# Gate and routing of the last batch ahead of the early experts, and four early experts in place of eight

## The chip, the cores and the metric

The kernel runs on one core of one Trainium2 chip. The metric is the device time of one execution in microseconds; the time of a kernel is the median of its runs. The core has five engines with a queue each, which run their instructions in the order of the program: TensorE (PE, matrix products and transposes), VectorE (DVE), ScalarE (ACT), GpSimd (POOL) and SyncE (SP). Transfers are issued by SP, ACT or POOL. A transfer with row numbers (an indirect gather or scatter) is issued by POOL.

## What is computed

Four batches of 512 tokens with 512 features pass through four layers, each added to its input. The first two are a quantized expert layer and a feed-forward layer whose weights come out of a table of 16 values. The third is a selective scan over the sequence: for each batch and feature it runs a recurrence with 16 states along the tokens, and the result is multiplied by a gate made from the normalized `x`. The fourth, which the change concerns, is a mixture of 32 experts:

```
probs = softmax(x @ gate_w)
w, sel = top_k(probs, 8);  w = w / sum(w)
pos = position of each (token, expert) pair within its expert, in order of tokens
t_slot, w_slot = token and weight of each slot of each expert
xg = x_pad[t_slot]
y  = (silu(xg @ w_gate[e]) * (xg @ w_up[e])) @ w_down[e]
out[t_slot] += w_slot * y
```

Each expert has matrices of 512x192 (gate and up) and 192x512 (down). With 2048 tokens and 8 experts for each there are 16384 pairs, 512 on average for an expert.

## The kernel before

`tile_kernel` writes the program from Python generators. `weave` takes steps of several generators in turn, in proportion to a number of steps given for each, so that their instructions are mixed in the order of the program. From that order a scheduler at build time makes the queue of each engine. It takes an instruction that stands later in the program when it reckons an engine to be free before an earlier one is ready. On the chip each queue runs in the order so made, and an instruction that waits holds up all that stand behind it on its engine.

The feed-forward layer and the scan of the batches fill the time up to about 1079 us. Batch `b`'s gate (`gate`, L599) and routing (`route`, L696) come once its scan is over, mixed with the scan of batch `b + 1`. For the last batch there is no later scan.

- `gate`: statistics of `x`, per feature block a normalization and a tanh on ACT (L607, L609) and two products on DVE (L610, L612), then transposes on PE (L616, tile `pt_y`) and an addition into `x` on DVE (L618). Statistics (`ln_stats`, L96) end on POOL, with a power and a product (L108, L109).
- `route`, first part: statistics, then four turns, one for every 128 tokens. Each normalizes on ACT (L705, by `normalize` at L114, tile `xn_r`, with a single buffer), stores the rows to the table `xln` in memory (L708, issued by SP), stores `x` to `kept` (L709), transposes on PE (L712), copies on ACT (L714), makes the logits on PE (L717) and copies them on ACT (L724).
- `route`, second part: softmax and the eight largest on DVE (L732 to L755), and the weights to `xln` (L758).
- `place` (L761): positions by products with a triangle and with ones (L772, L773), then four turns that make a table of slots: ACT copies (L795), DVE compares (L797, L804), ACT scales (L811), PE multiplies 32 small blocks (L814), DVE adds into the table (L821).
- `slots` (L826) and `slot_tokens` (L845) turn the tables into row numbers on DVE (L840, L842, L856 to L859). The gathers of the experts read these.

Tables are two: one for the tokens of the first two batches, one for those of the last two. The first `EARLY` experts are visited twice: once with up to 320 slots of the first half's tokens, for which batches 2 and 3 needn't be routed, and a second time with up to 320 slots of the second half's. All other experts have one visit with up to 576 slots, with tokens of both halves. A flag and a branch at the end do the layer again in full if the room was too small.

`expert` (L872) has four steps: SP loads the weights (`egu`, L881 to L883; `ed`, L888 and L890; three buffers) and POOL gathers the rows (L895, tile `xg`, ten buffers, 128 rows each); ACT copies the weights of the rows (L911, `gates`) and PE transposes them (L908, copied by ACT and DVE at L910); PE makes gate and up (L920, tile `pg`), and ACT and DVE the activation (L936 to L938, `eh`); PE makes the down projection (L949, L953, `po_e`), ACT or DVE weights it (L962, L960, `ey`), and POOL scatters it with addition into two tables `sums` (L963). `pipeline` (L972) runs these so that the loads of one expert, the transposes of the next and the products of another are mixed.

After the last scan the early experts' first visits are mixed with the last gate and routing, over the same PSUM banks as the scan (two banks for gate and up, two for transposes and down projections). Then the banks are laid out anew (four and four), and the late list begins, with the experts after `EARLY` in full and the second visits put between them; the last `LAST` = 2 second visits stand at the end, where the sums are read back and added to `x` (`add_sums`, L988).

Of the kernel before, what the change touches and what calls it, by code (L numbers as in the profile page):

```python
# [28 lines left out]
NB = 4  # L29
# [4 lines left out]
KH = HID // P  # L34
# [12 lines left out]


SLOTS = 576
EARLY = 8  # L50
ROOM = (320, 320)
AHEAD = 7
LAST = 2
# [8 lines left out]
class Kernel:  # L62
# [560 lines left out]
    def routing_constants(self, rp):  # L623
# [32 lines left out]
        for g, n in enumerate(ROOM):  # L656
            nc.vector.memset(self.room[:, g, :EARLY], float(n))
        self.no_row = c.tile([P, 1], F32, name="no_row", bufs=1)
# [37 lines left out]
    def route(self, rp, b):  # L696
# [53 lines left out]
        if b == NB // 2:  # L750
            nc.vector.memset(self.seen[0][:, :EARLY], 0.0)

# [275 lines left out]
def run(steps):  # L1028
    for _ in steps:
        pass  # L1030


def staggered(gens, starts):

    gens = list(zip(starts, gens))
    step = 0
    while gens:
        for g in [g for g in gens if g[0] <= step]:
            if next(g[1], StopIteration) is StopIteration:
                gens.remove(g)  # L1040
            else:
                yield
        step += 1


def weave(*streams):

    streams = [[0, n, g] for g, n in streams]
    while streams:
        s = min(streams, key=lambda s: s[0] / s[1])  # L1050
        s[0] += 1
        if next(s[2], StopIteration) is StopIteration:
            streams.remove(s)


@with_exitstack
def tile_kernel(ctx: ExitStack, tc: tile.TileContext, t: dict):
    k = Kernel(tc, t)
    k.constants(ctx)
    scan = ExitStack()  # L1060
    with ExitStack() as early:
        with ExitStack() as ffn:
            wp = ffn.enter_context(tc.tile_pool(name="wp", bufs=1, side="right"))
            with ExitStack() as first:
                k.banks(first, t=2, m=2, y=2, d=2)
                ap = first.enter_context(tc.tile_pool(name="ap", bufs=2))
                sq = staggered([k.smooth_quant(ap, b) for b in range(NB)], (0, 8, 23, 38))
                with ExitStack() as lut:
                    lc = lut.enter_context(tc.tile_pool(name="lc", bufs=1, side="right"))
                    lp = lut.enter_context(tc.tile_pool(name="lp", bufs=2, side="right"))  # L1070
                    k.lut_tables(lc, wp)
                    lookups = k.lut_weights(lp, k.jobs)
                    weave((islice(sq, 49), 49), (islice(lookups, 48), 48))
                    k.tile_rows(wp, lc)
                    weave((islice(sq, 59), 59), (lookups, 4 * len(k.jobs) - 48), (k.scratch(lc), 18))

                pp = ffn.enter_context(tc.tile_pool(name="pp", bufs=1, side="right"))
                k.scan_weights(pp)
                k.prep_tag = "y"
                preps = 2 * KH + 1  # L1080
                weave((k.prepare(pp, pp, 0), preps), (sq, 33))
            k.banks(early, t=2, m=2, y=1, d=3)
            k.prep_tag = "t"
            bp = ffn.enter_context(tc.tile_pool(name="bp", bufs=2, side="right"))
            rp = ctx.enter_context(tc.tile_pool(name="rp", bufs=1))
            mp = scan.enter_context(tc.tile_pool(name="mp", bufs=2))
            k.routing_constants(rp)
            steps = (TPB // 2) * (NIC + 3)
            units = KH * 16
            routes = 2 * (TPB + 1)  # L1090

            ffn_ = chain(*(k.lut_ffn(bp, b) for b in range(NB)))
            run(islice(ffn_, 4))
            for b in range(NB):
                n = steps
                streams = [(k.scan(mp, b), units), (islice(ffn_, n), n)]
                if b + 1 < NB:
                    streams.append((k.prepare(pp, (pp, mp)[(b + 1) % 2], b + 1), preps))
                if b:
                    run(k.gate(mp, b - 1))  # L1100
                    streams.append((k.route(rp, b - 1), routes))
                if b == NB - 1:
                    tok = k.slots(rp, k.tables[:1], 0, EARLY, ROOM[0], "a")
                    at = k.slot_tokens(rp, tok, ROOM[0], "a")
                weave(*streams)
        ep = ctx.enter_context(tc.tile_pool(name="ep", bufs=2, side="right"))
        k.gu_tag = "m"
        full, nc = SLOTS // P, tc.nc
        two = [k.sums[j % 2] for j in range(full + 1)]
        first = k.pipeline(k.expert(ep, e, (k.xln[0], *at, 0), e, ROOM[0], two) for e in range(EARLY))  # L1110
        weave((chain(k.gate(mp, NB - 1), k.route(rp, NB - 1)), KH + routes), (first, 2 * EARLY))
    scan.close()
    k.banks(ctx, t=4, g=4)
    k.gu_tag = "g"
    tp = ctx.enter_context(tc.tile_pool(name="tp", bufs=6))
    at = k.slot_tokens(rp, k.slots(rp, k.tables, EARLY, NE, SLOTS, "u"), SLOTS, "u")
    at_b = k.slot_tokens(rp, k.slots(rp, k.tables[1:], 0, EARLY, ROOM[1], "b"), ROOM[1], "b")
    k.overflow(rp)
    calls = [(e, at, e - EARLY, SLOTS) for e in range(EARLY, NE)]
    for e in range(EARLY - LAST):  # L1120
        calls.insert(2 * e + 1, (e, at_b, e, ROOM[1]))

    calls += [(e, at_b, e, ROOM[1]) for e in range(EARLY - LAST, EARLY)]
    sums = [two] * (len(calls) - LAST) + [k.sums[2:] * 3] * LAST
    late = k.pipeline(
        k.expert(ep, e, (k.xln[1], *at, 0), col, n, s) for (e, at, col, n), s in zip(calls, sums)
    )
    run(islice(late, 2 * (len(calls) - LAST)))
    weave(
        (late, 2 * LAST),  # L1130
        (
            chain(k.add_sums(tp, k.sums[:2], 0, NT // 2, True), k.add_sums(tp, k.sums[:2], NT // 2, NT, False)),
            NT // 2,
        ),
    )
    run(k.add_sums(tp, k.sums[2:], NT // 2, NT, True))
    more = nc.values_load(k.more[0:1, 0:1], min_val=0, max_val=1)
    with tc.If(more):
        k.in_full(rp, ep, tp)
# [51 lines left out]
```

## Time and profile before

| what | value |
|---|---|
| median of 3 runs | 1939.13 us (1932.53 to 1949.87) |
| the profiled execution's own time | 1929.09 us |
| its span, first to last instruction | 1926.9 us |
| mean granted clock of TensorE | 0.939 |
| PE busy with products | 1654.5 us, 86% of the span |
| DVE, ACT, POOL busy | 60%, 37%, 51% |
| transfers | 351.94 MB, 183 GB/s |

The profile is of one execution. Busy times are those of instructions that compute; a PE product's end is modelled. "PEld" is the load of the stationary operand, which overlaps products. `L920` is line 920. In a line of the timeline, the first two numbers are start and length in us, "x16" the number of instructions merged into it, and the brackets hold the idle time of the engine just before it and what ended that. Where a line stands for several, its length is that of the whole group. The granted clock is a share of full speed.

### The profile page before, as it was taken

The page shows a single profiled execution, that of the slowest core. Times are in us where ns is not written, and L with a number is a line of the kernel's source. Part 1 is how long each engine was busy: PE and PEld are TensorE (multiplying, and loading weights), DVE is VectorE, ACT ScalarE, POOL GpSimd, SP SyncE. Part 2 cuts the span into 40 slices and gives each one's busy share as a digit, 9 for nine tenths or more (in the row PEclk, how much of TensorE's full clock was granted, in tenths as well). Part 3 has the DMA queues.
Part 4 walks back from the last instruction along what each step waited for, and adds up shares of the span by engine and source line. Part 5 has one row for each costly group of instructions (what it writes and reads, how often), then busy time and mean ns, then how long its engine had stood idle before and what let it go on. Part 6 is the DMA issues. An engine that isn't in the chain of part 4 may idle for free. (4 is left out here: it accounts for less than half of the span.)

```text
span 1926.9 us, 25051 instructions
## 1 busy us (share of the span) xinstructions
PE 1654.5 (86%) x8845; PEld 981.0 (51%) x8845; DVE 1164.4 (60%) x2025; ACT 715.7 (37%) x1361; POOL 990.0 (51%) x844
## 2 busy tenths in 40 slices
PE   5778775798979898889799588899999999999981
PEld 3444332555455655455555244455656566665640
DVE  6877974688799879888889533523222223232333
ACT  1554555535444554355433332222222222222210
POOL 3110213768746775578466542456555555555421
PEclk9979996899999998999899699899999999999995
DMA  8525620889888788778899785688887777778766
GB/s 246 158 89 178 219 61 35 216 200 221 219 211 202 193 230 213 191 192 226 202 221 220 182 219 127 154 190 185 180 184 172 184 172 166 161 171 190 148 156 223
DMA packets 190363, 351.94 MB, mean 183 GB/s; under 512 B 41827, under 2 KB 88259, under 8 KB 190229
## 3 DMA queue, kind: packets, MB, share of 16 engines
q1 hardware_dynamic: 147844, 253.00, 48.9%
q0 software_dynamic: 39952, 92.66, 23.9%
q10 hardware_dynamic: 2432, 4.59, 0.7%
q8 instruction: 72, 1.18, 0.3%
q14 instruction: 63, 0.51, 0.1%
HBM read 279.17 MB, written 79.47 MB: 186 GB/s over the span
## 5 line engine op out<-in xcount | busy, mean ns | idle before, releaser
L963 POOL DMA_INDIRECT sums<-ey,to x168 | 261.6, 1557 | 299.9 <-DMA sums<-ey,to 122.6
L920 PE MATMUL pg<-exT,egu 128*128 128x320 f32 (+1 forms) x1536 | 403.4, 421 | 10.0 <-DVE exT L910 4.6
L569 POOL TENSOR_TENSOR dBu<-d,BC 128x512 f32<-128x512 f32 x256 | 325.7, 1280 | 118.1 <-DMA d<-dts 67.1
L920 PEld LDWEIGHTS pg<-exT,egu 128*128 128x128 f32 x1536 | 291.3, 193 | 125.8 <-issue 34.7
L574 DVE TENSOR_TENSOR_SCAN st<-st,dBu 128x512 f32<-128x512 f32 x192 | 230.4, 1216 | 37.8 <-POOL dBu L569 36.3
L567 ACT ACTIVATE st<-d,A 128x512 f32<-128x512 f32 x256 | 174.2, 690 | 195.8 <-DVE sc L575 118.8
L895 POOL DMA_INDIRECT xg<-xln,tokens x168 | 162.1, 965 | 101.1 <-PE pt_g L908 43.2
L381 PE MATMUL pgu<-xT,wg 128*128 128x256 f32 (+1 forms) x704 | 182.3, 401 | 15.8 <-DVE h L391 11.2
L937 DVE SCALAR_TENSOR_TENSOR eh<-eh,pg 64x128 f32<-64x128 f32 (+5 forms) x144 | 61.2, 425 | 214.9 <-ACT eh L936 213.8
L949 PE MATMUL po_e<-ed,eh 128*128 128x512 f32 (+1 forms) x336 | 171.3, 630 | 17.8 <-DVE eh L938 9.4
L381 PE MATMUL pgu<-xT,wu 128*128 128x256 f32 (+1 forms) x704 | 177.4, 394 | 0.0
L346 PE MATMUL pw<-oh,lut_t 128*32 128x344 bf16 (+1 forms) x2052 | 126.2, 363 | 58.4 <-DVE oh L340 58.0
L962 ACT ACTIVATE ey<-po_e,gates 128x512 f32<-128x512 f32 (+1 forms) x104 | 68.7, 684 | 281.1 <-PE po_e L953 140.8
L381 PEld LDWEIGHTS pgu<-xT,wg 128*128 128x128 f32 (+1 forms) x704 | 130.4, 195 | 78.9 <-issue 29.9
L960 DVE TENSOR_SCALAR ey<-po_e,gates 128x512 f32<-128x512 f32 x64 | 45.8, 747 | 204.5 <-PE po_e L953 204.5
L397 PE MATMUL po_f<-wd,h 128*128 128x512 f32 (+1 forms) x352 | 157.6, 603 | 2.7 <-DVE h L391 2.2
L381 PEld LDWEIGHTS pgu<-xT,wu 128*128 128x128 f32 (+1 forms) x704 | 135.8, 195 | 25.0 <-issue 4.2
L575 DVE TENSOR_TENSOR sc<-st,BC 128x512 f32<-128x512 f32 x192 | 127.4, 680 | 22.7 <-PE py L585 21.9
L579 POOL TENSOR_TENSOR sc<-sc,BC 128x512 f32<-128x512 f32 x64 | 81.7, 1276 | 100.2 <-DVE sc L572 75.7
L936 ACT ACTIVATE eh<-pg 64x128 f32<-64x128 f32 (+5 forms) x144 | 54.5, 384 | 157.3 <-PE pg L920 144.0
L953 PE MATMUL po_e<-ed,eh 64*128 64x512 f32 (+1 forms) x336 | 112.8, 635 | 0.0
L346 PEld LDWEIGHTS <-lut_t 128*32 128x32 bf16 x2052 | 57.5, 104 | 104.7 <-issue 58.4
(259 smaller groups left out, 2177.7 us busy)
## 6 DMA issues: line engine op xcount, KB each, us to landing
d<-dts SPq DMA_DIRECT2D x256, 512.0 KB, 6.4
egu<-in_w_gate SPq DMA_DIRECT2D x40, 384.0 KB, 4.2
sums<-zero SPq DMA_DIRECT2D x16, 768.0 KB, 6.5
ix<-idx_b SPq DMA_DIRECT2D x16, 688.0 KB, 6.0
egu<-in_w_up SPq DMA_DIRECT2D x40, 256.0 KB, 5.6
ed<-in_w_down SPq DMA_DIRECT2D x40, 256.0 KB, 3.8
ed<-in_w_down SPq DMA_DIRECT2D x80, 128.0 KB, 3.7
acc<-sums SPq DMA_DIRECT2D x20, 512.0 KB, 9.4
```

The costliest lines, as they stand in the source:

```text
L346: nc.tensor.matmul(pt[i][32 * c : 32 * c + 32, :step], lhsT=self.lut_t[:, j, g, :], rhs=oh[:, c * n + i * step : c * n + (i + 1) * step], ...
L381: nc.tensor.matmul(pg[:m, j * W : (j + 1) * W], lhsT=w[:, k, c * P : c * P + m], rhs=xT[:, k, :], start=k == 0, stop=k == KH - 1,)
L397: nc.tensor.matmul(po, lhsT=h[:m, c, i * P : (i + 1) * P], rhs=self.wd[:m, c, :], start=c == 0, stop=c == NIC - 1,)
L567: nc.scalar.activation(st, d[:, 0, :], AF.Exp, scale=self.A[:, i : i + 1])
L569: product = nc.gpsimd.tensor_tensor(dBu, d[:, 1, :], BC[:, 0, :], ALU.mult)
L574: nc.vector.tensor_tensor_scan(st, st, dBu, 0.0, ALU.mult, ALU.add)
L575: nc.vector.tensor_tensor(sc, st, BC[:, 1, :], ALU.mult)
L895: nc.gpsimd.indirect_dma_start(out=xg[:m, :], out_offset=None, in_=xln, in_offset=bass.IndirectOffsetOnAxis(ap=tokens[:m, lo + j, col : co ...
L920: nc.tensor.matmul(pg[i][:, :hs], lhsT=w[:, k, i * P : (i + 1) * P], rhs=xT[:, k, z : z + hs], start=k == 0, stop=k == KH - 1,)
L949: nc.tensor.matmul(po[j][:m, :], lhsT=h[:, 0, b : b + m], rhs=wd[:, 0, :], start=True, stop=False)
L953: nc.tensor.matmul(po[j][:m, :], lhsT=h[r : r + R, 1, b : b + m], rhs=wd[r : r + R, 1, :], start=False, stop=True)
L963: nc.gpsimd.indirect_dma_start(out=sums[j], out_offset=bass.IndirectOffsetOnAxis(ap=to[:m, lo + j, col : col + 1], axis=0), in_=y[:m, :], ...
```

## The change

`EARLY` is 4 and not 8, and the gate and the routing of the last batch stand wholly before the early experts in the program, in place of being woven with them.

```diff
-EARLY = 8
+EARLY = 4
@@
         two = [k.sums[j % 2] for j in range(full + 1)]
         first = k.pipeline(k.expert(ep, e, (k.xln[0], *at, 0), e, ROOM[0], two) for e in range(EARLY))
-        weave((chain(k.gate(mp, NB - 1), k.route(rp, NB - 1)), KH + routes), (first, 2 * EARLY))
+
+        run(chain(k.gate(mp, NB - 1), k.route(rp, NB - 1), first))
```

`EARLY` is also the number of second visits and the first expert of the late list, so experts 4 to 7 change from two visits of 320 slots to one of 576. The late list then has 28 full visits and 4 second ones, where it had 24 and 8. Of the second visits two stand between the first full ones and two at the end (six and two before).

The scheduler still puts some of the early experts' instructions ahead of later routing. In the changed program, PE has all of gate and routing first; ten transposes of the first early expert stand before the 32 blocks of the last table turn, and no other expert product stands ahead of these. ACT has nine copies of `gates` (L911), for the first three experts, ahead of the first normalization of routing. POOL has ten gathers ahead of the power (L108) of the routing's statistics. SP has the loads of experts 0 and, in part, 1 first, then the four stores to `kept`, the rest of expert 1's loads and those of expert 2 between the four stores of normalized rows.

## The prediction

> **What bounds the kernel now.** I read the page's slices first: TensorE (PE) is nine tenths busy or more from slice 27 to 38, after a dip just past the middle. Then I cut the span at the stages the change touches, and read there the chain of waits, the order on each engine, and the transfers.
>
> ```profile
> PE   5778775798979898889799588899999999999981
> PEclk9979996899999998999899699899999999999995
> ```
>
> That dip (slice 23 is 5 tenths, the next three 8) is the edit's place: the scan has ended and the experts start. Busy time by stretch (columns: stretch, length, PE, PEld, DVE, ACT, POOL, granted clock, DMA share, GB/s):
>
> ```profile
> 1079.00:1098.40 19.40, 6.08 (x25) 3.07 (x26) 8.12 (x15) 7.25 (x14) 11.28 (x12) 0.50 0.68 178
> 1098.40:1236.00 137.60, 119.57 (x572) 65.15 (x572) 56.43 (x171) 38.38 (x96) 51.30 (x42) 0.96 0.72 173
> 1256.50:1468.90 212.40, 210.21 (x825) 124.26 (x824) 61.49 (x122) 57.88 (x153) 121.69 (x98) 1.00 0.83 184
> 1468.90:1840.00 371.10, 371.10 (x1485) 228.21 (x1484) 108.20 (x203) 93.30 (x250) 209.04 (x165) 1.00 0.77 168
> ```
>
> From 1256 PE is the only bound: 371.10 of 371.10 us, then 86.9 us of tail. So the late experts cost exactly their PE time. The chain of waits gives the pitch:
>
> ```profile
> 1396.54 1.91 PE po_e L949 x4
> ...
> 1431.36 1.91 PE po_e L949 x4
> ...
> 1600.51 1.91 PE po_e L949 x4
> ...
> 1622.43 1.92 PE po_e L949 x4
> ```
>
> A full expert (576 slots) takes 1622.43 - 1600.51 = 21.92 us; a full one and a second visit of 320 slots take 1431.36 - 1396.54 = 34.82, so a second visit is 12.90. Before that, the timeline of PE:
>
> ```profile
> 1084.12 1.12 PE L616 MATMUL pt_y<-ident,u 128*128 128x128 f32 x4 [2.75 <-DVE u L612]
> ...
> 1098.44 7.22 PE L920 MATMUL pg<-exT,egu 128*128 128x320 f32 x16
> ...
> 1109.36 1.98 PE L949 MATMUL po_e<-ed,eh 128*128 128x512 f32 x4
> ...
> 1115.73 4.47 PE L920 MATMUL pg<-exT,egu 128*128 128x320 f32 x16
> ...
> 1225.84 1.98 PE L949 MATMUL po_e<-ed,eh 128*128 128x512 f32 x4 [0.28 <-DVE eh L938]
> ...
> 1235.46 0.16 PE L868 MATMUL pc<-flag,ones 128*128 128x1 bf16 x1 [3.73 <-ACT ey L962]
> ```
>
> The eight early experts start at 1098.44 and their down projections (L949) run from 1109.36 to 1225.84; gate and routing hide between them. The first late down projection is at 1256.48 by the same timeline. That is my yardstick.
>
> **The change, part by part.** *Late list.* Experts 4 to 7 lose both their early visit and their second visit of 320, and get one visit of 576 instead. Late: 4 x (21.92 - 12.90) = +36.1 us, all on the path, since nothing but PE binds there. The two small waits at the ends of pairs (0.49 us at 1355.9, 1.71 at 1462.3) may come once and not twice: -1. A row of full experts doesn't make POOL the bound: 5 gathers at 1.26 and 5 scatters at 1.87 (durations with the 0.3 us between issues) are 15.7 of 21.9 us, and the stretch from 1468.90 is just such a row.
>
> *Early stage.* In the changed program's order, PE has all gate and routing ahead of every expert but for ten transposes slipped in before the last of the four table turns. So routing, hidden till now, stands on the path alone. Its chain by the durations of before:
>
> - Gate: up to 1084.12 nothing changes. The last L612 ends at 1089.7; it is pushed by two adds of 0.68 (L618) that move ahead of it, then come transposes (1.12) and the last add: 1092. Statistics (four L103 and L104 at about 0.7, two L106/L107): 1095.
> - The power on POOL (L108, 1.04, and L109, 0.20) is queued behind ten gathers. The tenth ended at 1098.45 in before, so 1099.8, and not 1096.3.
> - ACT has nine gate copies (L911) ahead of the first normalization (L114), and each waits for its gather; the ninth in before was at
>
> ```profile
> 1104.26 0.19 ACT L911 COPY gates<-xg 64x1 f32<-64x1 f32 x1
> ```
>
>   which had an operation of ACT before it, so it is an upper mark. I take 1104; the bounds are 1099.8 and 1106, the latter if the four stores of x (1 MB) slow the gathers.
> - Four turns: L114 0.81, transposes 0.66, copy L714 0.59, logits L717 1.08, copy L724 0.19, with hops 3.6 us at full clock. Each also has a store of the normalized row (L708), whose buffer is single: its landing (2.0, 4.3, 7.6 us: least, median, most) is hidden when short, and the next turn waits when long.
>
> Here the skill speaks against the change. The Trainium skill, page "TensorE: Matmul & The Clock Gate", section "HAM oscillation — how this bites in real kernels", warns that PE gaps above about 3.4 us halve its clock. The trace agrees in kind: 0.50 over 1079 to 1098.4, where the four transposes took 1.12 and not 0.66. With such gaps in every stage of routing I take half clock throughout: 0.46 more on transposes and an estimated 0.8 on logits, 4.9 a turn, 19.6 in all (14.3 at full clock). Logits end at 1123.6. The experts' cold start is priced by the row: 16 matmuls 7.22 against 4.47, 2.75 us, where the page's 3.4 us at half rate would make it 1.7 (an estimate). Before pays it too, so it cancels.
>
> - Softmax and top eight: 1172.27 to 1178.12 in before, less 1.77 of expert operations between: 4.1. Positions (L772 to L790): 1.8 + 1.9. 1131.4.
> - Four table turns, serial on DVE, ACT and PE: L797 1.23, L804 0.75, L811 0.77, 0.51 from L814's start to L821, L821 0.30, hops 0.3 = 3.9; with one first copy (L795) and one expert copy (0.69) 16.4. Routing ends at 1147.8.
>
> So PE, which in before began the experts at 1098.44, begins at 1147.8: 49.4 later. L840's 3.5 us on DVE then lie ahead of the first L937; the cold first projection covers most of that (0 to 4 us; I take 0).
>
> *Four experts.* First down projection 10.92 later (1109.36 - 1098.44): 1158.7. The pitch of before is (1225.84 - 1109.36) / 7 = 16.64; without the gate's and routing's PE work in it (12 transposes 2.0, 16 transposes 2.6, logits 4.0, positions and tables 1.9: 10.5, or 1.5 an expert) 15.1. The fourth is at 1158.7 + 45.3 - 1.9, for the fifth's transposes that are gone: 1202.1.
>
> *Handover.* In before PE waited 3.73 + 0.84 + 0.83 + 0.43 us here, because slots and gathers came only after routing, and part of the work was cold: 30.6 from the last early L949 to the first late one. In the change slots and tokens are ready near 1153, so the handover costs its work: down projection 5.9, bank wait 0.8, transposes 2.3, gate and up 11.9, next transposes 1.4, hops 0.6 = 22.9. First late down projection at 1225.0, against 1256.5: -31.5 us.
>
> *Sum.* -31.5 + 36.1 - 1 = +3.6. On the profiled execution of 1929.1 us (span 1926.9 and 2.2 around it) this is 1932.7; the median of the runs, 1939.1, lies 10.0 above that execution, so 1943 in its terms. Everything before 1079 keeps its order on every engine; smaller copies of the four experts' slots (L842) are worth under 1 us.
>
> **Rivals.**
>
> *Transfers hold routing (slower).* On SP's queue nine weight loads of experts 1 and 2 stand between the four stores L708. In before, SP issues of such loads took 3.07 and 4.83 us (at 1090.4 and 1098.3) instead of 0.5, with 290 GB/s moving. Should each cost 2 us more and every turn wait for its store: +18, 1961. Against it: by 1104 only 3.1 MB of loads and stores and 2.4 MB of gathers (by their tiles) are asked for, which from 1085 at about 285 GB/s take 19 us, to 1104, just as the first store comes. It decides beyond 1% from 16 us on, turns of 8.9 and not 4.9.
>
> *Routing is short (same, a little faster).* Full clock (-5.3) and no wait for the ninth gather (-4.2): 1933.
>
> *The experts do slip into routing (faster).* If PE took the four experts' 60 us into routing's gaps, 40 of the 49.4 would come back: 1903. The orders of PE, ACT and DVE exclude it but for the ten transposes.
>
> **How the numbers follow.** My case 0.55; transfers 0.24; short routing 0.17; overlap 0.04. A measurement of this kernel tells about 1% from no change (three runs lie within 1932.5 to 1949.9), so within 1% is 1919.7 to 1958.5. My case runs from -4 to +12 around its value by the gather, clock and DVE bounds and the runs' spread, nearly all within 1%. Of the transfer case 0.20 and of mine 0.06 lie above: slower 0.26; the overlap and 0.03 of short routing below: faster 0.07; same 0.67. The range, 1926 to 1964, takes in short routing and the transfer case at its price, and leaves out the overlap.
>
> **What would show it.** First L114 of the last batch near 1104, directly after a gate copy; its turns near 4.9 us at clock 0.50; last L821 near 1147; first L920 right behind it, cold; no wait at the handover; first late L949 near 1225; the late pitch unchanged at 21.92, for 28 full and 4 second visits. Turns of 7 us or more, with ACT waiting on the xn_r store, would prove the transfer rival; PE busy with L920 before 1140 the overlap. I am wrong at the root if the late pitch changes.

## The result, and the profile after

The changed kernel takes 1953.09 us (median of 20 runs, 1948.55 to 1962.92) and the kernel before, run beside it, 1940.8 us (20 runs, 1931.49 to 1950.25): a ratio of 1.0068, 95% interval 1.0052 to 1.0084. That is 12.3 us slower, clear of the noise, yet within the 1% that the forecast called the same, and 10 us over the forecast time. The profiled execution took 1951.25 us, with a span of 1949.3. It is 22.2 us longer than the profiled one of the kernel before, which lay 11.7 us under its own median.

The sum of the forecast was +3.6 us. The trace says where the rest came from. First the slices of the page after:

```profile
PE   5778775898889988898889359999999999999981
PEclk9889995999989998999899569999999999999995
```

Slices 23 and 24 were 5 and 8 tenths and are now 3 and 5: routing stands alone on the path, at a granted clock of 5 and 6 tenths. The early stage in PE's timeline (start, length, engine, line, output and inputs, number of instructions; in brackets the idle time ahead and what ended it):

```profile
1089.19 1.11 PE L616 MATMUL pt_y<-ident,u 128*128 128x128 f32 x4 [2.75 <-DVE u L612]
...
1108.39 1.12 PE L712 MATMUL pt_r<-ident,xn_r 128*128 128x128 f32 x4 [11.97 <-ACT xn_r L114]
1110.19 1.91 PE L717 MATMUL pl<-gate_w,xT_r 128*128 128x32 f32 x8 [0.68 <-ACT xT_r L714]
1113.09 1.11 PE L712 MATMUL pt_r<-ident,xn_r 128*128 128x128 f32 x4 [0.99 <-ACT xn_r L114]
...
1140.10 0.39 PE L814 MATMUL pt_s<-hi_i,lo_i 128*32 128x18 f16 x32 [3.06 <-ACT hi_i L811]
1143.54 0.39 PE L814 MATMUL pt_s<-hi_i,lo_i 128*32 128x18 f16 x32 [3.06 <-ACT hi_i L811]
...
1149.95 6.67 PE L920 MATMUL pg<-exT,egu 128*128 128x320 f32 x16
1156.46 0.38 PE L908 MATMUL pt_g<-ident,xg 128*128 128x128 f32 x2
1159.01 2.39 PE L920 MATMUL pg<-exT,egu 128*128 128x320 f32 x8 [2.17 <-issue]
1161.24 0.99 PE L908 MATMUL pt_g<-ident,xg 128*128 128x128 f32 x8
1162.69 1.98 PE L949 MATMUL po_e<-ed,eh 128*128 128x512 f32 x4 [0.46 <-ACT exT L910]
...
1226.93 1.98 PE L949 MATMUL po_e<-ed,eh 128*128 128x512 f32 x4
```

The gate's transposes start at 1089.19, where the kernel before had 1084.12. These 5.07 us lie in the scan: its products (L585) were 5 us late by the 193rd of 512, at 648.74 where the kernel before had 643.73, far ahead of what the change moves. I take them off below, but that the change has no part in them is not shown. The seven profiles with four early experts, here and below, have this point at 1083.6 to 1091.2 (mean 1087.9), the seven with eight at 1079.2 to 1086.3 (mean 1084.0); what makes that difference stays open. From the gate to the first late down projection it is 1226.93 - 1089.19 = 137.74 us, against 1256.48 - 1084.12 = 172.36 before: the early stage is 34.6 us shorter.

The late list, from its first down projection to its last, takes 679.8 us against 628.4: 51.4 longer, where the prediction had 36.1 - 1 = 35.1. With 0.5 at the end of the program the parts make up the span: 5.1 - 34.6 + 51.4 + 0.5 = 22.4 = 1949.3 - 1926.9. The late list's share shows by stretch. Busy time (columns: stretch, length, PE, PEld, DVE, ACT, POOL, granted clock, DMA share, GB/s):

```profile
1306.00:1490.00 184.00, 181.46 (x714) 109.14 (x712) 51.83 (x97) 43.75 (x120) 102.61 (x82) 0.99 0.76 166
1490.00:1575.00 85.00, 85.00 (x346) 53.33 (x344) 25.19 (x48) 22.22 (x60) 48.74 (x40) 1.00 0.80 170
1575.00:1850.00 275.00, 270.39 (x1074) 163.69 (x1074) 78.44 (x146) 66.51 (x182) 149.13 (x118) 1.00 0.75 164
```

Between 1490 and 1575 PE is as full as it was before. On both sides of that it idles, 2.5 and 4.6 us, and the pitch of the full experts is not 21.92 but 21.99 to 25.76. The longest of these holds two losses, as PE's timeline has it:

```profile
1450.10 4.54 PE L920 MATMUL pg<-exT,egu 128*128 128x320 f32 x16 [0.40 <-DVE eh L938]
...
1474.16 6.24 PE L920 MATMUL pg<-exT,egu 128*128 128x320 f32 x16 [1.91 <-DVE eh L938]
```

PE waits for 1.91 us, and then the same 16 products take 1.70 longer: the granted clock is 0.73 over them (1474.16 to 1480.40), 0.50 in the two microseconds from 1476 to 1478, and 1.00 over the whole stretch from 1443 to 1474. Then the good stretch follows. The cause of the waits stands in POOL's timeline. First an expert in the good stretch, then one in the bad; each answer starts with the scatter of an expert's first block:

```profile
1531.29 1.63 POOL L963 DMA_INDIRECT sums<-ey,to  x1 [0.30 <-issue]
1536.86 1.58 POOL L963 DMA_INDIRECT sums<-ey,to  x1 [3.94 <-DMA sums<-ey,to]
1538.74 1.57 POOL L963 DMA_INDIRECT sums<-ey,to  x1 [0.30 <-DVE eh L938]
1542.54 1.44 POOL L963 DMA_INDIRECT sums<-ey,to  x1 [2.23 <-ACT eh L936]
1544.83 1.56 POOL L963 DMA_INDIRECT sums<-ey,to  x1 [0.86 <-issue]
1546.88 1.02 POOL L895 DMA_INDIRECT xg<-xln,tokens  x1 [0.48 <-PE pt_g L908]
...
1553.19 1.64 POOL L963 DMA_INDIRECT sums<-ey,to  x1 [0.30 <-issue]
```

```profile
1643.86 1.63 POOL L963 DMA_INDIRECT sums<-ey,to  x1 [0.30 <-issue]
1650.79 1.58 POOL L963 DMA_INDIRECT sums<-ey,to  x1 [5.30 <-DMA sums<-ey,to]
1652.67 1.57 POOL L963 DMA_INDIRECT sums<-ey,to  x1 [0.30 <-DVE eh L938]
1656.45 1.44 POOL L963 DMA_INDIRECT sums<-ey,to  x1 [2.22 <-DMA sums<-ey,to]
1658.63 1.56 POOL L963 DMA_INDIRECT sums<-ey,to  x1 [0.74 <-DMA sums<-ey,to]
1660.50 1.02 POOL L895 DMA_INDIRECT xg<-xln,tokens  x1 [0.31 <-PE po_e L949]
...
1666.83 1.65 POOL L963 DMA_INDIRECT sums<-ey,to  x1 [0.30 <-issue]
```

The five blocks of an expert are scattered in the order 0, 2, 1, 4, 3, and block `j` goes to table `j % 2`. So scatter 2 adds to the table that scatter 0 is still adding to, and POOL's queue stands still until that has landed: 3.94 us in the good stretch, 5.30 in the bad one. All that follows on POOL moves with it, and ends with no slack: the first gather waits 0.48 us in the one, which is 0.18 over the 0.30 between any two issues, and 0.31 in the other. The cycle is 1553.19 - 1531.29 = 21.90 us in the good stretch and 1666.83 - 1643.86 = 22.97 in the bad. PE gets the delay by way of ACT, whose fifth weighting needs the `ey` buffer that scatter 0 still reads:

```profile
1650.12 0.68 ACT L962 ACTIVATE ey<-po_e,gates 64x512 f32<-64x512 f32 x1 [9.76 <-DMA sums<-ey,to]
...
1651.31 1.09 ACT L936 ACTIVATE eh<-pg 64x256 f32<-64x256 f32 x3
```

The tanh of the next expert (L936) stands behind it on ACT, and PE's next projection waits for that activation (1.15 us, ended by `eh` L938, at 1652.73).

### The profile page after: what moved, and what is told of

It reads as the page before. It is cut to its first block, busy times and chain, and to the rows that moved or that the text cites. A ratio compares the mean times of both kernels' runs of the same rounds, so it can differ in the third digit from the quotient of the medians.

```text
span 1949.3 us, 24880 instructions
## 1 busy us (share of the span) xinstructions
PE 1651.4 (85%) x8803; PEld 986.0 (51%) x8813; DVE 1162.1 (60%) x2009; ACT 705.1 (36%) x1341; POOL 980.3 (50%) x836
## 5 line engine op out<-in xcount | busy, mean ns | idle before, releaser
L963 POOL DMA_INDIRECT sums<-ey,to x164 | 255.9, 1560 | 308.2 <-DMA sums<-ey,to 156.3
L895 POOL DMA_INDIRECT xg<-xln,tokens x164 | 158.1, 964 | 121.5 <-ACT exT L910 41.5
L937 DVE SCALAR_TENSOR_TENSOR eh<-eh,pg 128x320 f32<-128x320 f32 (+5 forms) x136 | 59.4, 437 | 235.9 <-ACT eh L936 234.3
L381 PE MATMUL pgu<-xT,wg 128*128 128x256 f32 (+1 forms) x704 | 184.1, 403 | 15.7 <-DVE h L391 11.0
L949 PE MATMUL po_e<-ed,eh 128*128 128x512 f32 (+1 forms) x328 | 165.9, 626 | 15.1 <-DVE eh L938 11.4
L575 DVE TENSOR_TENSOR sc<-st,BC 128x512 f32<-128x512 f32 x192 | 127.4, 679 | 23.0 <-PE py L585 22.1
L397 PEld LDWEIGHTS po_f<-wd,h 128*128 128x128 f32 (+1 forms) x352 | 67.8, 195 | 87.8 <-issue 82.2
L953 PE MATMUL po_e<-ed,eh 64*128 64x512 f32 (+1 forms) x328 | 108.5, 635 | 0.0
```

Source lines behind the costliest of these rows:

```text
L381: nc.tensor.matmul(pg[:m, j * W : (j + 1) * W], lhsT=w[:, k, c * P : c * P + m], rhs=xT[:, k, :], start=k == 0, stop=k == KH - 1,)
L397: nc.tensor.matmul(po, lhsT=h[:m, c, i * P : (i + 1) * P], rhs=self.wd[:m, c, :], start=c == 0, stop=c == NIC - 1,)
L575: nc.vector.tensor_tensor(sc, st, BC[:, 1, :], ALU.mult)
L895: nc.gpsimd.indirect_dma_start(out=xg[:m, :], out_offset=None, in_=xln, in_offset=bass.IndirectOffsetOnAxis(ap=tokens[:m, lo + j, col : co ...
L949: nc.tensor.matmul(po[j][:m, :], lhsT=h[:, 0, b : b + m], rhs=wd[:, 0, :], start=True, stop=False)
L953: nc.tensor.matmul(po[j][:m, :], lhsT=h[r : r + R, 1, b : b + m], rhs=wd[r : r + R, 1, :], start=False, stop=True)
```

## The experiments

All kernels compute the whole result; none leaves anything out. "Late list" is the time from the first to the last late down projection, "pitch" that between full experts.

### Is it the same-table wait?

The changed kernel again, then the same alternation of tables in it and in the kernel before. The alternation gives each scatter the table that the scatter ahead of it on POOL did not use; the number of scatters and the work stay:

```diff
-    sums = [two] * (len(calls) - LAST) + [k.sums[2:] * 3] * LAST
+    turn, sums = 0, []
+    for _, _, _, m in calls[:-LAST]:
+        issue = (0, 2, 1, 4, 3) if m == SLOTS else (0, 1, 2)
+        use = [None] * len(issue)
+        for j in issue:
+            use[j] = k.sums[turn % 2]
+            turn += 1
+        sums.append(use)
+    sums += [k.sums[2:] * 3] * LAST
```

The changed kernel unchanged (`after_again`):

> The changed kernel once more, for a second profile beside the variants. If the late waits are its own (theory A: GpSimd's queue, which in a row of full experts needs about 22.4 us an expert with its waits for scatters into the same table, more than TensorE's 21.92), the late pitch again leaves 21.92 in a third or more of the full experts, and the excess over 36.1 us is 10 us or more; ratio to the kernel before 1.005 to 1.009. If they were chance in one execution (theory B), the excess is now under 3 us and the profiled span near 1931. First late down projection 34 to 35 us earlier, counted from the first gate transpose, by both.

Measured 1952.64 us (ratio to the kernel before 1.0075, 1.0047 to 1.0102), with waits in nearly every full expert, pitch 22.1 to 24.0, late list 687.5 us. The waits belong to the kernel and not to one execution. Its late list is again 51.4 us longer than that of the kernel before in a second profile (`base_again` below, 636.1).

The changed kernel with the alternation (`after_alt`):

> The changed kernel, but the scatters of the late list alternate strictly between the two tables in the order in which GpSimd issues them, so that each waits for the one before the last and not for the last. Theory A (waits for the same table in GpSimd's queue): the late excess falls below 4 us, the span to about 1932 to 1938, ratio to the kernel before 0.996 to 1.001. Theory B (chance, or slow transfers as such): nothing changes, ratio 1.005 to 1.009. Theory C (the buffers of the weighted rows, four, hold ScalarE, whatever the tables): little changes, 1.004 to 1.009.

Measured 1932.39 us (0.997, 0.9955 to 0.9984), pitch 21.92 throughout, late list 661.5 us. POOL's timeline of one expert:

```profile
1613.35 1.63 POOL L963 DMA_INDIRECT sums<-ey,to  x1 [0.30 <-issue]
1615.28 1.58 POOL L963 DMA_INDIRECT sums<-ey,to  x1 [0.30 <-issue]
1619.01 1.57 POOL L963 DMA_INDIRECT sums<-ey,to  x1 [2.15 <-DMA sums<-ey,to]
1623.93 1.45 POOL L963 DMA_INDIRECT sums<-ey,to  x1 [3.35 <-DMA sums<-ey,to]
```

The second scatter follows the first after 1.93 us instead of 5.6 to 6.9. The later ones still wait, but at the end of the queue's cycle there is now room: the gathers wait 2.11 us for PE at 1607.02, and not 0.48. The waits in the changed kernel are worth 1952.64 - 1932.39 = 20 us (14 to 27, an interval that I get by resampling the runs).

The kernel before with the same alternation (`before_alt`):

> The kernel before with the same alternation of tables. Theory A: its runs lie 11 us above its one profiled execution, which showed no late waits, so they have such waits too, though fewer: ratio 0.993 to 0.997. Theories B and C: 0.999 to 1.001. If the late waits come from the longer row of full experts alone, also 0.999 to 1.001, but then the changed kernel with the alternation gains and this one does not.

Measured 1930.95 us (0.9962, 0.9947 to 0.9977); the late list is 628.7 us. This is the pair that prices the change by itself: with the orders of tables that keep PE from waiting in both, it costs 1932.39 - 1930.95 = 1.4 us (-0.7 to 3.6 by resampling), which can't be told from nothing. The alternation itself gives 6.7 us here (1937.65 - 1930.95) and 20 in the changed kernel.

### The two halves of the change

Four early experts, but woven with gate and routing as before (`early4_woven`):

```diff
-        run(chain(k.gate(mp, NB - 1), k.route(rp, NB - 1), first))
+        weave((chain(k.gate(mp, NB - 1), k.route(rp, NB - 1)), KH + routes), (first, 2 * EARLY))
```

> One part of the change alone: four early experts, still woven with the last gate and routing. My theory: the late list costs 36 us plus the late waits of the changed kernel, and the early stage gives back more than with routing bare, as part of the experts hides in it: first late down projection about 44 us earlier than before (about 10 earlier than in the changed kernel), ratio 1.001 to 1.004. Rival: woven routing takes as long with four experts as the stage of the changed kernel, since routing is a serial chain that each woven expert delays; then no gain against the changed kernel, ratio 1.006 to 1.009.

Measured 1941.77 us (1.0008, 0.9988 to 1.0028), its early stage 135.7 us from the gate to the first late down projection. I had expected 10 us less than in the changed kernel's 137.7; it is 2. Four woven experts do run during routing, but with pitches of 25.2, 19.2 and 18.1 us, and the last is followed by a handover of 48.06, in which PE has too little to do until slots and gathers are there. So in the early stage of four experts the weave hides next to nothing. The late list, 682.7 us, has the waits too. The whole program is 10.9 us ahead of `after_again` by the medians, though, and the early stage explains 2 of that; the runs spread widely (1924.65 to 1957.05), and the rest is not explained.

Gate and routing first, but eight early experts (`order_only`):

```diff
-EARLY = 4
+EARLY = 8
```

> The other part of the change alone: gate and routing wholly first, eight early experts. Routing bare and eight experts at the bare pitch of 14.35: from the first gate transpose to the first late down projection 137.7 + 4 x 14.35 = 195 us, against 172.4 before: +22.7 us in the profile. The late list is that of the kernel before. Ratio 1.009 to 1.014, by both theories of the late waits; below 1.005 would mean that bare routing isn't the cost I read from the profile.

Measured 1961.88 us (4 runs; 1.0101, 1.0048 to 1.0153). The early stage takes 197.2 us where 195 was expected and 172.4 was had before: bare routing costs eight early experts 24.8 us (172.4 to 197.2). Its early pitch is 14.35, as in the changed kernel. The waits set in from the ninth expert of the late row. Four experts in place of eight then take 59.5 us from the early stage (197.2 - 137.7). To the late list they add 44.9 by these two profiles (679.8 - 634.9), both with waits, where the sum without waits was 35.1.

### The version that beats both

Four woven experts with the alternation (`woven4_alt`):

> Four early experts, woven, with the alternation of tables. By theory A the late waits go here too (the profile of the woven kernel without it has some 20 us of them), so the late pitch is 21.92 throughout; the early stage of that kernel is only 2 us shorter than the changed kernel's, so this lies 1 to 3 us below the changed kernel with alternation: ratio to the kernel before 0.994 to 0.998. If the woven kernel's wide spread of runs (1925 to 1957) has another cause than the late waits, it stays: 0.998 to 1.003.

Measured 1926.25 us (0.9928, 0.9905 to 0.9952), pitch 21.92 throughout. That is below the range that I had given, and 6.1 us under the changed kernel with the alternation where I had expected 1 to 3. The early stage is 3.6 us shorter than there (134.7 against 138.3); the rest is not explained.

### More or less of the suspected wait

Six `ey` buffers for four, so that ACT need not wait for scatter 0 (`after_ey6`):

```diff
-                y = ep.tile([P, HID], F32, tag="ey", name="ey", bufs=4)
+                y = ep.tile([P, HID], F32, tag="ey", name="ey", bufs=6)
```

> The changed kernel with six buffers for the weighted rows instead of four, same tables: ScalarE's fifth weighting no longer waits for the first scatter of its own expert. Theory A (GpSimd's queue is the limit): two more buffers only put off the waits, the pitch still leaves 21.92 late in the row, ratio to the kernel before 1.002 to 1.007. Theory C (the link from scatter to ScalarE is what stops TensorE, and the queue has room): pitch 21.92 throughout, ratio 0.996 to 0.999.

Measured 1945.6 us (1.0033, 1.0016 to 1.0049), late list 675.0 us: the waits come later and less often, and single pitches still reach 26.55. Buffers put off what the queue loses; they don't give it back.

All late scatters but those of the last two visits to one table (`after_one`):

```diff
-    sums = [two] * (len(calls) - LAST) + [k.sums[2:] * 3] * LAST
+    one = [k.sums[0]] * (full + 1)
+    sums = [one] * (len(calls) - LAST) + [k.sums[2:] * 3] * LAST
```

> The changed kernel with the suspected wait at its largest: all scatters of the late list but the last two visits' go to one table, so each waits for the one before. By theory A an expert then costs GpSimd's queue 5 gathers at 1.26 and 5 scatters at 5.2 (issue to landing), 32 us, and TensorE follows: full pitch 30 to 35 us, the program 250 to 370 us longer than the changed kernel. If the queue's waits had room (theories B and C), the pitch stays near 22 to 25 us and the program within 80 us.

Measured 2187.64 us in one execution, 235 above `after_again`, somewhat less than I had put. The pitch of most full experts is 30.2 to 31.0 us, and POOL's timeline spells it out:

```profile
1617.76 1.58 POOL L963 DMA_INDIRECT sums<-ey,to  x1 [3.77 <-DMA sums<-ey,to]
1623.43 1.56 POOL L963 DMA_INDIRECT sums<-ey,to  x1 [4.09 <-DMA sums<-ey,to]
1629.11 1.56 POOL L963 DMA_INDIRECT sums<-ey,to  x1 [4.12 <-DVE exT L910]
1634.71 1.43 POOL L963 DMA_INDIRECT sums<-ey,to  x1 [4.04 <-issue]
```

In these lines scatters to one table follow each other at 5.60 to 5.68 us; over the late list, from one scatter of an expert to its next, the median is 5.59 us and most lie between 5.4 and 5.8. That the program waits at all is a need: the page "DMA: Bandwidth & Descriptors" of the Trainium skill, section "Rules for kernel authors", says that an addition reads its destination and writes it later with nothing holding it in between, so that the next one has to wait for the first one's semaphore. It gives no price for the wait; here it is 5.6 us from one block of 128x512 values to the next.

### Why the kernel before escapes

The kernel before has a row of 18 full experts between its pairs and its end (the changed one 26), and the same scatters. Is it free of waits in other executions? The kernel before unchanged (`base_again`):

> The kernel before, unchanged, for a second profile of it: ratio 1.000, within 0.002. Its first profile was at the fast end of its runs and had no late waits; by theory A a common execution of it has 5 to 12 us of them in the row of full experts, by chance alone (theory B) as many in pairs as in that row.

Measured 1941.3 us (1.0, 0.9981 to 1.0019). I had expected 5 to 12 us of waits in the row of full experts; there is none, all stand at 21.91 to 21.93. Some 7 us of waits sit in the pairs (pitches of 21.13 where before has 16.74, and of 19.35, 19.55 and 18.48 where others have 18.08).

So is it the length of the row? The kernel before with all eight second visits moved behind its 24 full ones (`before_row`):

```diff
-    for e in range(EARLY - LAST):
-        calls.insert(2 * e + 1, (e, at_b, e, ROOM[1]))
-    calls += [(e, at_b, e, ROOM[1]) for e in range(EARLY - LAST, EARLY)]
+    calls += [(e, at_b, e, ROOM[1]) for e in range(EARLY)]
```

> The kernel before with its eight second visits all behind the 24 full visits, so that the full ones stand in one unbroken row from the start, as they nearly do in the changed kernel; the computation and the amounts are the same. If the unbroken row is what brings the late waits (GpSimd has no slack in it to catch up after a slow scatter, and each second visit gives it some), the pitch leaves 21.92 in the row for 6 us or more in sum, ratio to the kernel before 1.002 to 1.008. If the late waits hang on something else of the changed kernel (what the early stage leaves behind, four weights fewer in flight), the row stays at 21.92, ratio 0.997 to 1.001.

Measured 1929.43 us (0.9958, 0.994 to 0.9976): 24 full experts in a row at 21.92, no waits, and faster than the kernel before. The length of the row alone does not bring them, and my expectation was wrong again.

What was left is that the row has two ways to run, and stays in the one it is in. To test that, the same unbroken row gets one knock: POOL multiplies the five blocks of the ninth full expert by ones ahead of their scatters (`row_kick`), and the same with the alternation (`row_alt_kick`):

```diff
+                if e == 16:
+                    y4 = y[:m, :].rearrange("p (k w) -> p k w", k=KH)
+                    one = self.ones[:m, :].unsqueeze(1).to_broadcast([m, KH, P])
+                    nc.gpsimd.tensor_tensor(y4, y4, one, ALU.mult)
                 nc.gpsimd.indirect_dma_start(
```

> The kernel before with the unbroken row of 24 full experts (before_row), and in one of them, the ninth, POOL multiplies each of the five weighted blocks by ones ahead of its scatter: five instructions at an estimated 1.3 us, from the products of 128x512 on POOL in the scan, 6.4 us in all, once. Theory A, the waits keep themselves going once the row has been knocked out of step: from the ninth full expert on the pitch is over 22 us for most of the 15 that remain, PE and POOL waiting as in the changed kernel, and the time is 10 to 20 us above before_row (1929.4). Theory B, the row falls back by its slack of about 1 us an expert: at most 6.4 us lost at the ninth and tenth, then 21.92 again, at most 7 us in all; then something that lasts must hold the changed kernel in its waits.

> The same with the scatters alternating between the two tables in POOL's order. Theory A of the knock needs the wait for the same table to keep the row out of step: without it the pitch is back at 21.92 within three experts, and the time is within 5 us of before_row. If here too the pitch stays over 22 us to the end of the row, the same-table wait isn't what keeps it there.

Measured 1937.53 us for the first (0.9987, 0.9967 to 1.0006) and 1928.0 for the second (0.9936, 0.9915 to 0.9956). The pitches of the knocked row, from its second expert on (the last is 21.05 in `before_row`, since a shorter visit follows):

```
row_kick      21.92 (ten times) 22.86 22.81 23.61 22.04 22.15 23.45 23.76 22.20 22.00 22.13 22.11 23.00 21.69
row_alt_kick  21.92 throughout (21.91 to 21.93), the last 21.06
```

Up to the knock the row runs at 21.92. The gathered rows in stock carry PE over two more experts; then every one that is left is late, to the end of the row, 13 in all. They sum to 9.7 us in this execution. In the medians it is 8 us (1937.53 against 1929.43), or 6 when each is set against the runs of the kernel before that stood beside it, under the 10 to 20 that I had put. With the alternation the same knock costs nothing.

The loss is more than the knock put in. The five multiplications took 7.5 us, but mostly in time in which POOL stood waiting: from the scatter 0 ahead of the knock (1419.96) to the second one behind it (1465.89) are 45.93 us, where two experts take 43.84, so POOL fell back by 2.1 us. A queue with merely no slack would hand on these 2.1 us, and 1.3 or so more for a pause that this row has anyway (below), but 9.7 followed. So the late state keeps itself going for a while, and the same-table wait is what keeps it.

POOL's timeline of the knocked row, before the knock and after it:

```profile
1419.96 1.61 POOL L967 DMA_INDIRECT sums<-ey,to  x1 [0.30 <-issue]
1425.69 1.58 POOL L967 DMA_INDIRECT sums<-ey,to  x1 [4.11 <-DMA sums<-ey,to]
...
1488.32 1.62 POOL L967 DMA_INDIRECT sums<-ey,to  x1 [0.30 <-issue]
1495.07 1.58 POOL L967 DMA_INDIRECT sums<-ey,to  x1 [5.13 <-DMA sums<-ey,to]
```

From scatter 0 to the next it is 5.73 us ahead of the knock and 6.75 behind it. SP's timeline tells what differs: it issues the loads of the next down projection's weights (L888) when PE has freed their buffer, so by PE's time, while scatter 0 comes by POOL's. In step, the load came 3.09 us after scatter 0; behind the knock 0.49 us after it:

```profile
1423.05 0.34 SPq L888 DMA_DIRECT2D ed<-in_w_down  x1
...
1488.81 0.34 SPq L888 DMA_DIRECT2D ed<-in_w_down  x1
```

The same reading over the late rows of eight profiles without the alternation (before, after, `after_again`, `base_again`, `before_row`, `order_only`, `early4_woven`, `row_kick`):

| load L888 issued | full experts | scatter 0 to the next scatter, median | least and most |
|---|---|---|---|
| 2.9 to 3.3 us after scatter 0 (in step) | 60 | 5.64 us | 5.34 to 7.18 |
| 1.3 to 2.9 us after it | 30 | 5.65 us | 5.39 to 6.91 |
| 1.2 before to 1.0 us after it (POOL late) | 77 | 6.54 us | 5.95 to 8.08 |

(The 13 experts left out stand at the end of the list.) Of the 30 in the middle the four with the load at 1.3 to 1.5 us have 6.5 to 6.9 us, the others, with one exception, at most 5.9. So where POOL is late by about 1.6 us or more against PE, its scatter also lands some 0.9 us later, more than the few tenths that it can catch up in an expert (the knock-free part of the row took back 0.32 us, 1376.73 to 1398.33, after a slow landing of 6.26). The way back shows in the changed kernel: ahead of its longest wait of PE the load came 0.52 us before scatter 0 (1465.28), behind it 2.10 after (1488.42), and the good stretch followed. That the load is what delays the scatter is likely, and not shown: no run moved the load alone, and other transfers that follow PE's time move with it.

What gives the first knock in the changed kernel? In its two profiles it is the first full expert after the second pair, with 6.49 us (at 1306.63) and 6.29 (at 1306.10) from scatter 0 to the next, though the load was in step; in `after_ey6` and `early4_woven`, which have the same list, POOL's cycle there is 22.9 and 23.2 us long, too. In before and `base_again` the corresponding cycle takes 21.9 and 22.1.

A part of the knock has a fixed place in the list. In that expert the fifth scatter follows the fourth after 3.89 us (1318.55 to 1322.44), and after 3.77, 3.68 and 3.46 in the other three profiles; six visits later it is 3.3 to 3.4 in all four. In the other full experts of the changed kernel's profile it is 1.75 to 2.54. A wait for the same table it is not: the scatter ahead of it to that table had landed at 1320.32. With the list of the kernel before (before, `base_again`, `order_only`) the one such place is the third full expert from the end (3.3 to 3.9), where little can follow. `before_row` has it in its sixteenth of 24 (3.18) and took it back. What POOL does in these 1.3 us or so the profiles don't show, and no run moved them.

A slow landing in the middle of the row can come ahead of the late state as well: 7.18 us at 1575.12 ended the good stretch of the changed kernel, 6.95 at 1629.23 began the bad one of `order_only`. What makes these landings slow is not known. So why the kernel before escapes is answered in part: its row has no such place until its end, and the slow landings in it, up to 6.32 us in two profiles, were taken back.

## Why the prediction was right, and where it was not

The time lies in the range, the sign and the class are as forecast. By the steps, with the 5.07 us of the scan taken off the times after:

| step | predicted | after, less 5.07 |
|---|---|---|
| gate's last add ends | 1092 | 1092.1 |
| POOL's L108, L109 behind ten gathers, end | 1099.8 | 1099.8 |
| first L114, behind nine gate copies on ACT | 1104 (1099.8 to 1106) | 1102.5 |
| a routing turn | 4.9 | 4.69 to 4.75 |
| logits end | 1123.6 | 1121.5 |
| positions end | 1131.4 | 1128.5 |
| a table turn | 3.9 | 3.44 |
| routing ends (last L821) | 1147.8 | 1144.3 |
| first early down projection | 1158.7 | 1157.6 |
| fourth | 1202.1 | 1199.7 |
| handover | 22.9 | 22.15 |
| first late down projection | 1225.0 | 1221.9 |

**The queues held as read from the program's order.** ACT's timeline has the ninth gate copy and the first normalization back to back:

```profile
1107.43 0.19 ACT L911 COPY gates<-xg 64x1 f32<-64x1 f32 x1 [0.52 <-DMA xg<-xln,tokens]
1107.53 0.81 ACT L114 ACTIVATE xn_r<-x,ln_off,ln_rs 128x512 f32<-128x512 f32 x1
```

The mark of 1104 was 1.5 us too high, as the prediction had said an upper mark may be: here ACT stood waiting for the gather itself (0.52 us).

**Half clock in routing was right.** Transposes took 1.12 us and the logits 1.91; the estimate was 1.12 and 1.08 + 0.8. The granted clock over 1088 to 1146 is 0.50. The cold start of the experts came to 6.67 us against 4.57 for the warm 16 matmuls, 2.1 us: between the row of before (2.75) and the prediction's estimate of 1.7 from the page "TensorE: Matmul & The Clock Gate" of the Trainium skill, section "What's actually happening", which has the first 3.4 us or so of work at half clock.

**Small terms.** Positions and softmax took 7.0 us for 7.8, table turns 3.44 for 3.9, the early pitch 14.35 for 15.1. Against that, the slots and row numbers on DVE (L840 to L859), put at 0 of 0 to 4, cost a wait of 2.17 us in the first projection: PE goes on at 1159.01, when L938 has ended behind them (1158.91). Together the early stage gave 34.6 and not 31.5.

**The transfer rival fell**, with a chance of 0.24: no turn waits for its store. A normalization follows the logits copy directly (1112.22 after the copy at 1112.13), and SP's issues in routing took 0.32 to 0.63 us each. **The short routing** was half right: no full clock, but 1.5 us of the gathers' wait. **No expert slipped in**: PE's first expert transposes are at 1144.55, just before the last table turn, as the order said.

**The step that failed** is the late list: "all on the path, since nothing but PE binds there", and the claim that a row of full experts doesn't make POOL the bound, with 15.7 of 21.9 us. I had named a changed late pitch as what would prove me wrong at the root, and it did change, from 21.92 to mostly 22.0 to 23.4. The 15.7 us counted what POOL does and not what it waits for. In the good cycle from 1531.29 POOL stands a further 3.6, 1.9 and 0.6 us beyond the 0.3 between issues: 15.7 + 6.1 = 21.8 of 21.9. Two of the three brackets name an activation or nothing, but these scatters come 5.57, 5.68 and 6.09 us after the one ahead of each to the same table, about what scatters to one table take in `after_one`. The profile of before showed it. POOL's timeline of one expert there, and the lines of the two pages (busy time and mean, then idle time ahead and what ended most of it; before, then after):

```profile
1605.42 1.62 POOL L963 DMA_INDIRECT sums<-ey,to  x1 [0.30 <-issue]
1611.01 1.58 POOL L963 DMA_INDIRECT sums<-ey,to  x1 [3.97 <-DMA sums<-ey,to]
...
1621.01 1.02 POOL L895 DMA_INDIRECT xg<-xln,tokens  x1 [0.76 <-PE pt_g L908]
```

```profile
L963 POOL DMA_INDIRECT sums<-ey,to x168 | 261.6, 1557 | 299.9 <-DMA sums<-ey,to 122.6
L963 POOL DMA_INDIRECT sums<-ey,to x164 | 255.9, 1560 | 308.2 <-DMA sums<-ey,to 156.3
```

The first gather had 0.76 - 0.30 = 0.46 us to spare, in a stretch in which PE never waited; I took POOL's idle time as proof of room. The term that was mis-sized is the late list's +35.1, which measured +51.4 in both pairs of profiles. With the alternation in both kernels, and no waits of PE in their rows, it measures 661.5 - 628.7 = 32.8 (4.3 of the 628.7 are one wait at the start of the list), and the change costs 1.4 us by the medians, where the sum with its early stage as measured (-34.6 + 35.1) gives +0.5 and as predicted +3.6. So the forecast was near for the parts that it priced. The other 11 to 14 us (12.3 or, by `after_again`, 15.0, less 1.4) are waits that it ruled out. That they fell inside its range was luck: the range had been drawn for the transfer rival.

## What to carry to other kernels

Count an in-order queue's waits, not only its work, when you ask whether it can become the bound: an engine busy 50% can have no slack. Where scatters with addition go to several tables, let each go to another table than the one just ahead of it in the queue, and not in the blocks' order: here it gave 0.4 to 1%. A loop whose slack per turn is a few tenths of a us can hold two paces, and a delay of about 2 us can then cost many turns behind it, here up to the end of the row; compare pitches along the row before reading its mean.

## What the hardware showed that I had not expected

- Scatters with addition to one table follow one another at a median of 5.59 us (`after_one`, blocks of up to 128 rows of 512 values), all of it in POOL's queue; to another table the next is issued 1.93 us after the first (`after_alt`).
- A single delay of POOL by 2.1 us (`row_kick`) held up the 13 experts from the third after it to the end of the row, by 0.1 to 1.8 us each, 9.7 in all.
- A wait of PE of about 2 us in the row can cost more than itself. In the eight profiles of the table and `after_ey6`, 76 waits of 0.15 us or more stand ahead of the 16 products of a full expert's second half in the late list. The 70 of up to 1.89 us left these at 4.54 or 4.55 us. Of the six from 1.91 to 2.69 us, four were followed by 6.23 or 6.24 us at a granted clock of 0.73, and two (1.97 and 2.00, both in `early4_woven`) by 4.55 at 1.00. These gaps are shorter than the 3.4 us that the prediction went by.
- Weaving four early experts with routing makes the early stage only 2.0 us shorter than leaving routing bare (135.7 against 137.7 us), or 3.6 with the alternation in both; with eight it is 24.8 us (172.4 against 197.2).
